# First layer of a graph network: quarter sums in seven slots a block, late tiles summed with the next group

## The chip, the cores and the metric

The kernel runs on one core of a Trainium2 chip. The metric is the device time of the whole kernel in microseconds (us), lower is better. A core has a matrix engine (PE), a vector engine (DVE), a scalar engine (ACT), a general engine (POOL, which also issues indirect gathers) and a queue engine (SP); data come and go by DMA.

## What is computed

The reference is a chain of four residual steps over 6250 nodes of 256 features and 106250 directed edges, sorted by their target node: a graph layer with edge attributes, a mixture of four experts gated by graph attention, a second graph layer, a second mixture. The change touches the first step alone:

```python
def _L0_gnn_ref(x, edge_index, edge_attr, u, batch, W1, b1, W2, b2):
    row, col = (edge_index[0], edge_index[1])
    h = jnp.concatenate([x[row], edge_attr], axis=1)
    h = jax.nn.relu(h @ W1 + b1)
    agg = jax.ops.segment_sum(h, col, num_segments=N_NODES)
    cnt = jax.ops.segment_sum(jnp.ones((h.shape[0],), h.dtype), col, num_segments=N_NODES)
    agg = agg / jnp.maximum(cnt, 1.0)[:, None]
    out = jnp.concatenate([x, agg], axis=1)
    return jax.nn.relu(out @ W2 + b2)

x = x + _L0_gnn_ref(_layernorm(x, axis=-1), edge_index, edge_attr_256, ...)
x = x + _L0_ffn_ref(_layernorm(x, axis=-1)[None], ...)[0]
x = x + _L1_gnn_ref(_layernorm(x, axis=-1), edge_weight, ..., src, dst)
x = x + _L1_ffn_ref(_layernorm(x, axis=-1)[None], ...)[0]
```

Each edge thus needs one row of x times the upper half of W1, its own attributes times the lower half, a relu, and then a sum over the edges of each target.

## The kernel before

**Tiles.** The nodes are cut into 49 blocks ("windows" in the code) of 128. The edges of a window fill 18 tiles of 128 edges. These form six runs of three tiles (`NT = 3`), k = 0 to 5, and three groups: group g has the runs g and g + 3, six tiles (`G1 = 6`). There are 147 groups, `groups1`. The table `y_dram` holds x W1's upper half for every node, so that a row of it can be gathered for each edge.

**Summing with one-hot quarters.** A window's 128 target nodes are four quarters of 32. As the edges are sorted, the edges of a tile lie in a few of them. `QUARTERS` says for each run of three tiles which: (0, 1), (0, 2), (1, 3), (1, 4), (2, 4), (3, 4), that is 1, 2, 2, 3, 2 and 1 quarters, so 33 quarter sums in 18 tiles. Edges outside these ranges are kept apart by a mask (`inside`, L1224 to L1237) and treated elsewhere. `equal` (L1270) builds the one-hot matrix `eq` on DVE, and `add_up` (L1609) multiplies: each matmul is a 128 x 32 column tile, which sums one tile's 128 rows of 257 values (256 and a one for the count) into 32 partitions of the PSUM tile `pe`. Matmuls into different quarters can run side by side, up to four of them; such a set is called a slot here. Before, a window's 12, 12 and 9 quarter sums of its three groups lie in nine slots, three for each group. The last window has whole 128-wide sums instead.

**The loop.** Iteration q does, in this order and kept so by `ordered.pin()` on each engine:

- `join(q - 1)`: DVE adds the gathered rows to the hidden product in PSUM (L1586), ACT takes the relu in place (L1587).
- `hidden(q, 0)`, later `hidden(q, 2)` and `hidden(q, 4)`: PE multiplies the transposed attributes by the lower half of W1 (L1160, `ph<-w1b,et`), two tiles at a time.
- steps of other work: the sort of the edges for the later stages, and `end_of(w)` of windows already summed (L1619 to L1663 on DVE and ACT, L1154, L1155 and L1160 for the products).
- `add_up(q - 2)`: the sums of a group joined one iteration earlier.
- `load_sources(q + 2)`: six gathers `h<-y_dram,src` on POOL (L1173) into a ring of four row buffers. The slot that they write is the one that `add_up(q - 2)` has just read, and in which the relu of that group wrote. So the first of the six waits for the group's last sum; the others have nothing more to wait for from PE.
- `turn(q + 1)`: DVE transposes the attributes (L1568, `et<-ea`).
- `load_attr`: DMAs of the attributes, issued from SP and ACT (L1477).

`eq` has three buffers. A DMA instruction can carry one wait; further ones are put into a semaphore instruction ahead of it on the same engine. On POOL there are 383 such instructions in the whole program before, 956 with the change; PE has 336 matmuls fewer, and the streams of SP and DVE stay as they were but for the masks.

`lt` (L1411) is a small bf16 tile in a later helper that writes part of the sorted order to DRAM: six times, a copy on ACT and a store from it.

Of the kernel before, what the change touches and what calls it, by code (L numbers as in the profile page):

```python
# [9 lines left out]
F32 = mybir.dt.float32  # L10
I32 = mybir.dt.int32
AF = mybir.ActivationFunctionType
OP = mybir.AluOpType
# [4 lines left out]
P = 128  # L18
# [889 lines left out]
BF16 = mybir.dt.bfloat16  # L908
# [3 lines left out]
def kernel(ctx: ExitStack, tc: tile.TileContext, a: dict, out: bass.AP):  # L912
# [10 lines left out]
    N, D = a["x"].shape  # L923
    T = -(-N // P)
# [12 lines left out]
    CW = 18  # L937
# [53 lines left out]
    with ExitStack() as fast:  # L991
# [39 lines left out]
        src1 = edges.tile([P, T, NR, NT], I32, name="src1")  # L1031
# [140 lines left out]
        def gather(dst, table, idx):  # L1172
            GP.indirect_dma_start(  # L1173
                out=dst, out_offset=None, in_=table[0:NP, :],
                in_offset=IndirectOffsetOnAxis(ap=idx, axis=0),
            )

        def load_windows(b, pool):

            sl = slice(b * TB, (b + 1) * TB)  # L1180
            n = TB * CW

            def flat3(v):
                return v.rearrange("p w a t -> p w (a t)")

            raw = {k: wix.tile([P, P], I32, name=f"raw_{k}") for k in ("src", "dst")}
            for w in range(b * TB, (b + 1) * TB):
                at, r = (w - b * TB) * CW, start_of(w)
# [38 lines left out]

            n = TB - (b == NB - 1)
            for k, (lo, hi) in enumerate(QUARTERS):
                for limit, op in ((lo * Q - 0.5, OP.is_gt), (hi * Q - 0.5, OP.is_lt)):  # L1230
                    if 0 < limit < P - 1:
                        V.scalar_tensor_tensor(
                            inside[:, :n, k, :], d[:, :n, k, :], limit, inside[:, :n, k, :],
                            op0=op, op1=OP.mult,
                        )
            if n < TB:
                V.scalar_tensor_tensor(  # L1237
                    inside[:, n, :, :], d[:, n, :, :], LAST - 0.5, inside[:, n, :, :],
                    op0=OP.is_lt, op1=OP.mult,
                )  # L1240
# [15 lines left out]
        def equal(pool, w, q):  # L1256


            total = NT * Q * sum(hi - lo for lo, hi in (quarters(w, q), quarters(w, q + NG)))
            if w < T - 1:  # L1260
                eq = pool.tile([P, EQ], F32, name="eq", bufs=3)
            else:
                eq = pool.tile([P, total], F32, name="eq4", bufs=1)
            found, at = {}, 0
            for k in (q, q + NG):
                lo, hi = quarters(w, k)
                n = (hi - lo) * Q
# [118 lines left out]
        def sorted_edges(pst, wk):  # L1386
# [19 lines left out]
            for c in range(0, KA, P):  # L1406
                n = min(P, KA - c)
                pt = pst.tile([P, 4, P], F32, name="pt")
                TE.transpose(pt[0:n, 0, :], some[:, c : c + n], ident)
                lt = wk.tile([P, P], BF16, name="lt")  # L1410
                SC.activation(lt[0:n, :], pt[0:n, 0, :], AF.Copy)  # L1411
                SC.dma_start(low_dram[c : c + n, :], lt[0:n, :])
                if c % (2 * P):
                    yield
# [7 lines left out]
        with ExitStack() as layer:  # L1422
# [114 lines left out]
            with (  # L1537
# [12 lines left out]
                last_of = [  # L1550
                    max(k % NG for k, (lo, hi) in enumerate(QUARTERS) if lo <= b < hi)
                    for b in range(4)
                ]
# [12 lines left out]

# [22 lines left out]

                def add_up(q):  # L1590

                    w, g = groups1[q]
                    if g == 0:
                        sums[w] = pse.tile([P, WS], F32, name="pe")
                    h, eq = rows_of(q), equals.pop(q)

                    for j in reversed(range(NT)):
                        for i, k in ((1, g + NG), (0, g)):
                            lo, hi = quarters(w, k)
                            if hi - lo == 4:  # L1600
                                TE.matmul(
                                    sums[w], eq[k][:, j, :], h[:, i * NT + j, 0:WS],
                                    start=g == 0 and j == NT - 1 and i == 1,
                                    stop=g == NG - 1 and j == 0 and i == 0,
                                )
                                continue
                            for b in range(lo, hi):
                                at = slice((b - lo) * Q, (b - lo + 1) * Q)
                                TE.matmul(  # L1609
                                    sums[w][b * Q : (b + 1) * Q, :], eq[k][:, j, at],  # L1610
                                    h[:, i * NT + j, 0:WS], start=g == 0 and j == NT - 1,
                                    stop=g == last_of[b] and j == 0,
                                )

                def end_of(w):

# [1180 lines left out]
```

## Time and profile before

| | us |
|---|---|
| median of three runs | 4278.34 (4271.37 to 4294.4) |
| the profiled execution | 4285.28 |
| its span | 4283.5 |
| PE busy | 3272.3 (76%) |
| POOL busy | 2257.1 (53%) |
| DVE busy | 2166.2 (51%) |
| ACT busy | 1188.7 (28%) |
| add-ups of the first layer | from 125.8 to 1539.4 us of the span |

Durations below come from the profiled execution. Its span is what the engines' records cover, 1.8 us less than its time. Views used are the page of the whole execution, tables by stretches of time, groups of instructions by line, the sums of waits, and the timelines of single engines. In a group, "idle before" is the time for which the engine did nothing just ahead of an instruction of the group, and "<-" names what ended it; "issue" means that nothing which the profile shows was being waited for. A matmul of 32-bit floats leaves two records, so 24 records are 12 matmuls.

### The profile page before, as it was taken

Reading aid. Unit: us, or ns where it says so; the run is one execution under the profiler, and the core shown is the slowest. Engines: PE = TensorE matmul, PEld = TensorE weight load, DVE = VectorE, ACT = ScalarE, POOL = GpSimd, SP = SyncE. Lnnn points to the kernel's source line nnn. Section 1 sums busy time; section 2 is a strip of 40 time slices with the busy share of each in tenths; the row PEclk is TensorE's granted clock in tenths of the full one; section 3 lists DMA queues with packets and bytes.
Section 4 is the critical chain, followed back from the end, with each engine's and each line's share of the span. In section 5 each row is a group of like instructions: output and inputs, shape, how many; then the busy total and the mean of one; then the engine's idle time right before and its main releaser. Section 6 shows DMA issues by size and latency. Waiting matters only on the chain.

```text
span 4283.5 us, 59672 instructions
## 1 busy us (share of the span) xinstructions
PE 3272.3 (76%) x19189; PEld 2500.2 (58%) x19189; DVE 2166.2 (51%) x6247; ACT 1188.7 (28%) x2203; POOL 2257.1 (53%) x2720
## 2 busy tenths in 40 slices
PE   6798888888888785777887877785346777877787
PEld 4566666666666564566665666573244555555566
DVE  7576666666555444545463544575123333333344
ACT  4122222222222232334444343463011211211123
POOL 1655655566565544345454444422666666665651
PEclk9899999999999897888998988796567667677678
DMA  5677776777676642223333332343111111111110
GB/s 172 158 172 164 167 161 157 161 171 165 159 168 153 147 108 58 61 65 100 84 99 78 81 89 67 87 109 90 45 46 52 47 51 51 50 51 48 53 47 19
DMA packets 698942, 429.43 MB, mean 100 GB/s; under 512 B 530968, under 2 KB 639563, under 8 KB 698620
## 3 DMA queue, kind: packets, MB, share of 16 engines
q0 software_dynamic: 88512, 177.73, 17.3%
q1 hardware_dynamic: 366812, 188.25, 16.4%
q10 hardware_dynamic: 243296, 59.53, 7.0%
q8 instruction: 155, 2.54, 0.3%
q14 instruction: 167, 1.37, 0.1%
HBM read 382.75 MB, written 42.50 MB: 99 GB/s over the span
## 4 chain that ended last, share of the span: by engine, by line
PE 36%; another core or an unknown queue 14%; issue 6%; DVE 5%; ACT 3%; DMA 1%; POOL 1%; DVEq 0%; ACTq 0%; SPq 0%
PE ph L1160 13%; PE py L1160 11%; PE pe L2662 5%; PE pt L1160 2%; PE po L1986 2%; PE pa L1909 1%; DVE eq L2641 1%; POOL hg L1173 1%; DVE E L1964 1%; DVE x_all L2617 1%; ACT L1787 0%; ACT hh L1787 0%; PE pe L1609 0%; PE pt L1154 0%
## 5 line engine op out<-in xcount | busy, mean ns | idle before, releaser
L1173 POOL DMA_INDIRECT h<-y_dram,src x882 | 858.4, 973 | 669.0 <-issue 485.7
L1173 POOL DMA_INDIRECT hg<-hp_dram,src x831 | 784.9, 944 | 490.7 <-issue 225.0
L1173 POOL DMA_INDIRECT sg<-gat_dram,src x612 | 593.8, 970 | 723.1 <-DVE pay L1946 313.8
L1160 PE MATMUL ph<-w1b,et 128*128 128x256 f32 x3528 | 868.2, 398 | 32.8 <-issue 26.9
L1160 PEld LDWEIGHTS ph<-w1b,et 128*128 128x128 f32 x3528 | 680.3, 198 | 204.4 <-issue 114.3
L1160 PE MATMUL py<-w,hh 128*128 128x256 f32 x1568 | 454.0, 428 | 105.6 <-issue 54.5
L2662 PEld LDWEIGHTS pe<-eq,hg 128*128 128x128 f32 x2036 | 375.3, 261 | 189.8 <-issue 117.5
L2662 PE MATMUL pe<-eq,hg 128*128 128x96 f32 (+15 forms) x2036 | 386.4, 342 | 126.2 <-issue 67.2
L1586 DVE TENSOR_TENSOR h<-ph,h 128x1536 f32<-128x1536 f32 x147 | 258.2, 1757 | 421.1 <-remote 158.6
L1160 PE MATMUL ph<-b_all,w 128*128 128x256 f32 (+1 forms) x1600 | 458.9, 426 | 11.8 <-issue 11.5
L2641 DVE TENSOR_SCALAR eq<-px,dst,ew 128x96 f32<-128x96 f32 x831 | 261.1, 367 | 320.1 <-remote 131.4
L1587 ACT ACTIVATE h<-h 128x1536 f32<-128x1536 f32 x147 | 218.2, 1484 | 728.6 <-DMA ea<-in_edge_attr_dram 288.4
L1160 PEld LDWEIGHTS py<-w,hh 128*128 128x128 f32 x1568 | 308.1, 210 | 171.1 <-issue 70.2
L1160 PEld LDWEIGHTS ph<-b_all,w 128*128 128x128 f32 x1600 | 316.9, 214 | 55.5 <-issue 17.4
L1964 DVE TENSOR_SCALAR E<-nodes,bits 128x256 bf16<-128x256 bf16 (+5 forms) x612 | 187.6, 340 | 194.4 <-remote 73.3
L1609 PE MATMUL pe<-h,eq 128*32 128x257 f32 x3168 | 256.7, 416 | 36.3 <-issue 35.2
L1568 DVE STREAM_TRANSPOSE et<-ea 128x1536 f32<-128x1536 f32 x147 | 260.5, 1773 | 12.7 <-issue 9.3
L1787 ACT ACTIVATE hh<-ph,b 128x256 f32<-128x256 f32 (+1 forms) x400 | 166.5, 467 | 306.8 <-remote 166.5
L1160 PE MATMUL py<-ew,g 65*128 65x256 f32 x392 | 146.6, 503 | 57.5 <-DVE x_all L2617 42.1
L1609 PEld LDWEIGHTS pe<-h,eq 128*32 128x32 f32 x3168 | 104.7, 116 | 143.6 <-issue 91.1
L1986 PE MATMUL po<-pays,E 128*128 128x61 bf16 x2116 | 120.0, 199 | 48.1 <-issue 41.8
L1160 PE MATMUL ph<-b_all,ew 128*128 128x512 f32 (+2 forms) x256 | 115.4, 576 | 53.4 <-ACT g L2577 33.8
(355 smaller groups left out, 3971.7 us busy)
## 6 DMA issues: line engine op xcount, KB each, us to landing
ea<-in_edge_attr_dram ACTq DMA_DIRECT2D x588, 96.0 KB
ea<-in_edge_attr_dram SPq DMA_DIRECT2D x588, 96.0 KB
w<-in_L_ffn_W_dram SPq DMA_DIRECT2D x48, 512.0 KB
y<-ys SPq DMA_DIRECT2D x96, 256.0 KB
rb<-low_dram SPq DMA_DIRECT2D x84, 256.0 KB
h<-y_dram,src POOLq DMA_INDIRECT x882
hg<-hp_dram,src POOLq DMA_INDIRECT x831
gtab<-y SPq DMA_DIRECT2D x100, 128.0 KB
```

The source lines that it names most:

```text
L1160: TE.matmul(dst, lhs(c), rhs(c), start=c == 0, stop=c == n - 1)
L1173: GP.indirect_dma_start(out=dst, out_offset=None, in_=table[0:NP, :], in_offset=IndirectOffsetOnAxis(ap=idx, axis=0),)
L1568: V.transpose(et[q].rearrange("p c m k -> p m c k"), ahead.pop(q).rearrange("p i m (c k) -> p (i m) c k", c=2),)
L1586: V.tensor_add(h, ph.pop(q), h)
L1587: SC.activation(h, h, AF.Relu)
L1609: TE.matmul(sums[w][b * Q : (b + 1) * Q, :], eq[k][:, j, at], h[:, i * NT + j, 0:WS], start=g == 0 and j == NT - 1, stop=g == last_of[b] a ...
L1787: SC.activation(hidden[u][:, f, :n, :], ph[:, f - f0, :n, :], AF.Gelu, bias=b1[:, e, f : f + 1],)
L1909: TE.matmul(pas[g][:, j, 0 : n * H], rows[g][:, j, :], part[:, i, b0 : b0 + n, :].rearrange("p t h -> p (t h)"), start=i == 0, stop=i == 2,)
L1964: V.tensor_scalar(Es[g, j][:, 0:n, :].rearrange("p b k -> p (b k)"), nodes16[:, 0 : n * P], bits.bitcast(F32)[:, g * G + j : g * G + j + 1 ...
L1986: TE.matmul(pos[g][bank][:, to * HP : (to + 1) * HP], E[:, b - b0, :], pays[g % 2][:, j, :], start=bank not in begun, stop=bank not in lat ...
L2641: V.tensor_scalar(equals[k][:, j, :], lanes[:, 0:NW], dst_of[:, t : t + 1], ew[:, t : t + 1], op0=OP.is_equal, op1=OP.mult,)
L2662: TE.matmul(sums[b][:, lo - t0 * P : hi - t0 * P], hg[:, j, :], eq[:, j, lo - n0 : hi - n0], start=False, stop=after >= (t0 + n) * P,)
```

## The change

The set of quarters is given for each tile instead of for each run of three. `RANGES` lists it in order of the 18 tiles: 26 quarter sums instead of 33. The groups of a window are taken in the order 2, 0, 1 (`TURNS`) and have 2, 2 and 3 slots (`SLOTS`), seven in all. `planned` deals the quarter sums into slots; what does not fit is left for the window's next turn, and it may be left only from the two last tiles of the two runs of a group (`LATE1`, tiles 2 and 5). The turns so have 6, 8 and 12 matmuls. As rows and one-hots of the late tiles are still needed one iteration later, the gathers are split: `load_sources(q + 1, LATE1)` gathers the two late tiles of the next group, an iteration later than before, and `load_sources(q + 2, EARLY1)` the other four. `eq` has four buffers. `lt` has one buffer; the pool's default is two.

```diff
+    TURNS, SLOTS = (2, 0, 1), (2, 2, 3)
+    RANGES = (((0, 1), 3), ((0, 2), 2), ((1, 2), 2), ((1, 3), 3), ((2, 3), 1), ((2, 4), 3), ((3, 4), 4))
+    reach = [r for r, n in RANGES for _ in range(n)]
...
-            for k, (lo, hi) in enumerate(QUARTERS):
-                for limit, op in ((lo * Q - 0.5, OP.is_gt), (hi * Q - 0.5, OP.is_lt)):
-                    if 0 < limit < P - 1:
-                        V.scalar_tensor_tensor(
-                            inside[:, :n, k, :], d[:, :n, k, :], limit, inside[:, :n, k, :],
-                            op0=op, op1=OP.mult,
-                        )
+            for limit in range(1, 4):
+                for op, some in (
+                    (OP.is_gt, [j for j in range(CW) if reach[j][0] == limit]),
+                    (OP.is_lt, [j for j in range(CW) if reach[j][1] == limit]),
+                ):
+                    part = slice(some[0], some[-1] + 1)
+                    V.scalar_tensor_tensor(
+                        tiled[0][:, :n, part], tiled[1][:, :n, part], limit * Q - 0.5,
+                        tiled[0][:, :n, part], op0=op, op1=OP.mult,
+                    )
...
-                eq = pool.tile([P, EQ], F32, name="eq", bufs=3)
+                eq = pool.tile([P, EQ], F32, name="eq", bufs=4)
...
-                lt = wk.tile([P, P], BF16, name="lt")
+                lt = wk.tile([P, P], BF16, name="lt", bufs=1)
...
-            groups1 = [(w, g) for w in range(T) for g in range(NG)]
+            groups1 = [(w, g) for w in range(T) for g in TURNS]
...
+                def planned():
+
+                    left, plan, first, final = [[] for _ in range(4)], [], {}, {}
+                    for i, g in enumerate(TURNS):
+                        for j, (k, t) in enumerate(chunk(g)):
+                            for b in range(*reach[k * NT + t]):
+                                left[b].append((i, j, k, t))
+                        for n in range(SLOTS[i]):
+                            for b in range(4):
+                                if left[b]:
+                                    plan.append((i, b, *left[b].pop(0)))
...
-                def load_sources(q):
+                def load_sources(q, some):
...
-                        gather(rows_of(q)[:, j, 0:D], y_dram, src1[:, w, k, t : t + 1])
+                        if j in some:
+                            gather(rows_of(q)[:, j, 0:D], y_dram, src1[:, w, k, t : t + 1])
...
-                    for j in reversed(range(NT)):
-                        for i, k in ((1, g + NG), (0, g)):
-                            lo, hi = quarters(w, k)
...
-                            for b in range(lo, hi):
-                                at = slice((b - lo) * Q, (b - lo + 1) * Q)
-                                TE.matmul(
-                                    sums[w][b * Q : (b + 1) * Q, :], eq[k][:, j, at],
-                                    h[:, i * NT + j, 0:WS], start=g == 0 and j == NT - 1,
-                                    stop=g == last_of[b] and j == 0,
-                                )
...
+                    for i, b, own, j, k, t, start, stop in plan:
+                        if i == turn:
+                            of = q - turn + own
+                            lo = QUARTERS[k][0]
+                            TE.matmul(
+                                sums[w][b * Q : (b + 1) * Q, :],
+                                equals[of][k][:, t, (b - lo) * Q : (b - lo + 1) * Q],
+                                rows_of(of)[:, j, 0:WS], start=start, stop=stop,
+                            )
...
                 for q in range(3):
-                    load_sources(q)
+                    load_sources(q, range(G1))
...
+                    if 3 <= q + 1 < NQ1:
+                        load_sources(q + 1, LATE1)
                     if 3 <= q + 2 < NQ1:
-                        load_sources(q + 2)
+                        load_sources(q + 2, EARLY1)
```

More of the change, by code (lines that the diff above doesn't have):

```diff
@@ L1228, in load_windows @@
             n = TB - (b == NB - 1)
-            for k, (lo, hi) in enumerate(QUARTERS):
-                for limit, op in ((lo * Q - 0.5, OP.is_gt), (hi * Q - 0.5, OP.is_lt)):
-                    if 0 < limit < P - 1:
-                        V.scalar_tensor_tensor(
-                            inside[:, :n, k, :], d[:, :n, k, :], limit, inside[:, :n, k, :],
-                            op0=op, op1=OP.mult,
-                        )
+            tiled, at = (v.rearrange("p w a t -> p w (a t)") for v in (inside, d)), 0
+            tiled = list(tiled)
+            for limit in range(1, 4):
[4 more added lines that the diff above has]
+                    part = slice(some[0], some[-1] + 1)
+                    assert len(some) == some[-1] + 1 - some[0]
+                    V.scalar_tensor_tensor(
+                        tiled[0][:, :n, part], tiled[1][:, :n, part], limit * Q - 0.5,
+                        tiled[0][:, :n, part], op0=op, op1=OP.mult,
+                    )
             if n < TB:
@@ L1548 @@
                 equals, et, ph, sums = {}, {}, {}, {}
[L1550 to L1553, printed above, removed]
+                def planned():
[8 more added lines that the diff above has]
+                                    plan.append((i, b, *left[b].pop(0)))
+                        assert all(v[0] == i and v[1] in LATE1 for some in left for v in some)
+                    assert not any(left)
+                    for n, v in enumerate(plan):
+                        first.setdefault(v[1], n)
+                        final[v[1]] = n
+                    return [
+                        (*v, n == first[v[1]], n == final[v[1]]) for n, v in enumerate(plan)
+                    ]
+                LATE1 = (NT - 1, 2 * NT - 1)
+                EARLY1 = tuple(j for j in range(G1) if j not in LATE1)
+                plan = planned()
                 NQ1 = len(groups1)
@@ L1590, in add_up @@
                 def add_up(q):
-                    w, g = groups1[q]
-                    if g == 0:
+                    w, turn = groups1[q][0], q % NG
+                    if turn == 0:
                         sums[w] = pse.tile([P, WS], F32, name="pe")
-                    h, eq = rows_of(q), equals.pop(q)
-                    for j in reversed(range(NT)):
-                        for i, k in ((1, g + NG), (0, g)):
-                            lo, hi = quarters(w, k)
-                            if hi - lo == 4:
-                                TE.matmul(
-                                    sums[w], eq[k][:, j, :], h[:, i * NT + j, 0:WS],
-                                    start=g == 0 and j == NT - 1 and i == 1,
-                                    stop=g == NG - 1 and j == 0 and i == 0,
-                                )
-                                continue
-                            for b in range(lo, hi):
-                                at = slice((b - lo) * Q, (b - lo + 1) * Q)
-                                TE.matmul(
-                                    sums[w][b * Q : (b + 1) * Q, :], eq[k][:, j, at],
-                                    h[:, i * NT + j, 0:WS], start=g == 0 and j == NT - 1,
-                                    stop=g == last_of[b] and j == 0,
-                                )
+                    if w == T - 1:
+                        for j, (k, t) in enumerate(chunk(TURNS[turn])):
+                            TE.matmul(
+                                sums[w], equals[q][k][:, t, :], rows_of(q)[:, j, 0:WS],
+                                start=turn == 0 and j == 0, stop=turn == NG - 1 and j == G1 - 1,
+                            )
+                        return
+                    for i, b, own, j, k, t, start, stop in plan:
+                        if i == turn:
+                            of = q - turn + own
+                            lo = QUARTERS[k][0]
+                            TE.matmul(
+                                sums[w][b * Q : (b + 1) * Q, :],
+                                equals[of][k][:, t, (b - lo) * Q : (b - lo + 1) * Q],
+                                rows_of(of)[:, j, 0:WS], start=start, stop=stop,
+                            )
                 def end_of(w):
```

## The prediction

> **What bounds the kernel now.** The change touches the first layer only, so I first marked that stage in the timeline: the add-ups of 144 of the 147 groups lie between 125.8 and 1539.4 us of the span, 9.82 us a group. Next the table by windows for the flat part of the stage, then the groups of instructions by line for 130 to 1540 us, then the waits, then the timelines of PE and POOL over three quiet groups.
>
> The window table (length, then busy us and instruction count of PE, PE's loads, DVE, ACT and POOL, then clock, DMA share and GB/s):
> ```profile
> 200.00:1500.00 1300.00, 1108.41 (x6807) 823.74 (x6805) 794.85 (x1467) 293.91 (x493) 770.10 (x790) 0.92 0.71 162
> ```
> PE is busy 85% of the stage and POOL 59%, so at first sight PE is the bound. The groups by line say something else (busy us, mean ns, then idle us before the instruction, and what ended it):
> ```profile
> L1160 PE MATMUL ph<-w1b,et 128*128 128x256 f32 x3433 | 841.9, 397 | 23.8 <-issue 23.1
> L1173 POOL DMA_INDIRECT h<-y_dram,src x858 | 835.0, 973 | 574.9 <-issue 478.7 <-ACT o L1155 52.1 <-ACT b_all L1155 19.5
> L1609 PE MATMUL pe<-h,eq 128*32 128x257 f32 x3163 | 255.3, 416 | 36.3 <-issue 35.2 <-DMA h<-y_dram,src 0.8
> ```
> POOL's 858 gathers take 835.0 us, and the idle time before them is 574.9 us: together 1410, the whole stretch. One gather costs 0.973 us, and 574.9 us is far more than 858 small gaps. The timeline of POOL shows where it sits (start, length, and in brackets the idle time before):
> ```profile
> 881.63 0.95 POOL L1173 DMA_INDIRECT h<-y_dram,src  x1 [0.30 <-issue]
> 884.90 0.94 POOL L1173 DMA_INDIRECT h<-y_dram,src  x1 [2.33 <-issue]
> 886.15 0.95 POOL L1173 DMA_INDIRECT h<-y_dram,src  x1 [0.30 <-issue]
> ...
> 891.16 0.95 POOL L1173 DMA_INDIRECT h<-y_dram,src  x1 [0.30 <-issue]
> 894.39 1.00 POOL L1173 DMA_INDIRECT h<-y_dram,src  x1 [2.28 <-issue]
> ```
> Six gathers of 0.95 us, five gaps of 0.30 and one hole of 2.3 make 9.5 us, and this is the period of the groups here. The timeline of PE for the same groups:
> ```profile
> 881.37 1.51 PE L1609 MATMUL pe<-h,eq 128*32 128x257 f32 x24
> 882.81 3.72 PE L1160 MATMUL ph<-w1b,et 128*128 128x256 f32 x16
> ...
> 888.63 1.50 PE L1609 MATMUL pe<-h,eq 128*32 128x257 f32 x18
> 890.06 3.72 PE L1160 MATMUL ph<-w1b,et 128*128 128x256 f32 x16
> ...
> 896.11 1.51 PE L1609 MATMUL pe<-h,eq 128*32 128x257 f32 x24
> ```
> From add-up to add-up PE needs 7.26 and 7.48 us. The sum that the gather at 884.90 waits for ended at 882.88, 2.0 us before; that of 894.39 ended at 890.13, 4.3 us before. So POOL's own cadence, hole included, is slightly the slower of the two, and PE catches up and then stands. The hole is not there where POOL found its wait done on arrival:
> ```profile
> 804.39 0.95 POOL L1173 DMA_INDIRECT h<-y_dram,src  x1 [0.30 <-issue]
> ...
> 819.28 0.95 POOL L1173 DMA_INDIRECT h<-y_dram,src  x1 [7.68 <-ACT o L1155]
> ```
> The first line begins a group and has 0.30 before it; the second shows the other case, POOL really late because PE and ACT were. I sorted the 142 starts of groups: 22 have 0.30, some 30 start 0.77 to 0.80 us after the last sum they need (PE late, gaps 2.9 to 10.6), and the other 90 or so have the hole of 2.0 to 2.3.
>
> [...]12 quarters (24 records) take 1.51 us and 9 quarters (18 records) take 1.50, so what costs is the slot of up to four, 0.50 us, not the quarter. [...]
>
> **The change part by part.** 1. Slots: nine a window become seven, so two times 48 windows = 96 fewer (the last window keeps whole sums). Below, 1.50 / 3 = 0.50 us each: 48 us of PE. By the group's busy time 255.3 / 432 = 0.59: 57 us; by the shortest reading, 0.45: 43. I take 48, a third of a microsecond a group. PE's issued matmuls fall by 336 (33 to 26 quarters a window, seven times 48).
>
> 2. What of it reaches the end? In the 112 groups with a hole or with nothing late, POOL's cadence hides it: nothing. In the 30 where PE is late the next gathers start at once with PE's signal.
>
> 3. Waits of the gathers. Before, the first of six waits for the last sum of the group. After, each waits for the last sum of its own tile. The first gather of an iteration (a late tile) is released by the first of the slots, as the leftover tiles are summed first: two or so slots earlier, 1.0 us. 30 groups by 1.0 us = 30 us. This includes the shorter add-up, for the first release comes before the dropped slots. If PE is late again by as much in the next group it is not all kept; if a shorter add-up also lets the hidden matmuls behind it run sooner, more: 20 to 45.
>
> 4. What this adds on POOL: 573 more waiting instructions (semaphore instructions on POOL go from 383 to 956), since nearly every gather now needs both PE's signal and that of the gather eight before it, and one DMA instruction carries one of them. Where both are done, 0.30 us of gap is what a gather with a finished wait shows now: nothing. Where one is not, a hole of up to 2.3 us behind five finished gathers, or none: in the stage of the GAT, gathers that carry their wait on DVE themselves follow at 0.30 in the three places where the signal came during the run; in the second layer, gathers that carry a PE wait with one more wait ahead show both 0.30 and about 2.7. So from minus 2 to plus 2.3 us a blocked wait. I take zero: the hole stays once a group, as all sums of one add-up end within 1.5 us of each other, while a hole lasts longer.
>
> 5. Late tiles gathered one iteration later: two groups ahead instead of three. Their data land some 3 us (2.4 to 6) after the issue, and the joins are 8 to 19 us after a group's last gather now; one iteration is 9.8. Most keep some microseconds; nothing, with 0 to 15 us for groups where it is short.
>
> 6. The fourth buffer of eq costs nothing on any engine. The lt tile with one buffer instead of the pool's two makes six copies on ACT wait for the store before: five waits of up to 3 us at 1422 to 1437, in a stretch where ACT stands up to 12 us; 2 us, at most 15. The tests of the ranges: six operations of 0.175 us on DVE per seven windows instead of seven; nothing. SP's and ACT's DMAs of edge attributes are the same in number and order.
>
> Sum: -30 + 2 = -28. The profiled execution took 4285.28 us (span 4283.5), so 4257.3 there; it lies 6.9 us above the median of the runs, 4278.34, so against that 4250.
>
> **The rivals.** A, the sum above: 4250, own range 4225 to 4265. B, hidden: the 30 late groups are late through the chain PE, ACT, PE of the window's end (the 7.68 us above was released by ACT), and the earlier signal only makes POOL's hole longer: 4278, 4265 to 4285. For it speaks that the periods of 9.5 us follow POOL; against it, that 30 groups do start at PE's signal.
>
> C, slower: a second hole in a group. After the late pair is released, the wait of the third gather may not yet be done when POOL's queue comes to it, and it costs another 2.3 us. The place is the turn with 12 sums, where the two pairs' signals lie farthest apart. In a third of the groups, 48 x 2.3 = 110, less 30: 4358. From 13 groups on (30 / 2.3) it eats the gain, and in all 144 it would give 4580. For it: one wait more per gather and both kinds of gap in the second layer. Against it: in quiet groups the sums were done 2 to 6 us before the gathers.
>
> D, the hole goes: waits carried by the gathers themselves[...] let POOL find waits done. Cadence then falls to 6 x 1.25 = 7.5 us, and PE binds: 1108.41 / 1300 x 9.82 = 8.37 us a group, less 0.33, is 8.04, against 9.82: at most 256 us. The trace speaks against more than half of it: where the hole was missing, POOL ran twelve gathers and PE then stood some 9 us. I take 100: 4178.
>
> **How the numbers follow.** A 0.40, B 0.18, C 0.26, D 0.16; A is likeliest, so 4250. With 0.5% (21 us, about what a measurement of this kernel can tell from no change) as the bound, A gives faster in 0.33 and no change in 0.07, B no change, C slower, D faster: 0.49, 0.25, 0.26. The range, 4165 to 4335, holds A, B, two thirds of D and a third of C, about 0.78; A's own range stands above.
>
> **What would show it.** PE's sums at about 2490 records (two to a matmul) and 205 us in the stage, gathers still 0.97 us: step 1. Holes of 2.0 to 2.3 once a group and first gathers some 0.8 us after an early sum: steps 2 to 4 as I put them. Two holes a group, or holes in the middle of the six: C. Group starts at 0.30 and PE without standing: D. ACT or DVE waiting for the late gathers' data more than the 199.5 us that the relu shows now: step 5 was wrong. I am wrong mainly if the number of holes changes, since one hole (2.3 us) weighs as much as four to five slots.

## The result and the profile after

The changed kernel takes 4416.85 us (4409.29 to 4424.11), the kernel before, beside it, 4286.37 us (4271.37 to 4295.95): 1.0308 times, with an interval of 1.0267 to 1.0348. It is slower by some 130 us where 28 us less were forecast.

Nearly all of it is in the first layer. From the first to the last of 144 add-ups the kernel before needs 1412.1 us (125.8 to 1537.9, starts), the changed one 1546.2 us (122.4 to 1668.6). That is 134.1 of the 135.9 us by which the spans differ (4419.4 and 4283.5). I split the distance between starts of add-ups by their place in the window. Before, the means are 10.99, 7.47 and 11.20 us; after, 10.33, 6.97 and 15.23. So the first two distances of each window became shorter, by 0.66 and 0.50 us, together 56 us over 48 windows. The third, from the add-up of the third turn to the first of the next window, became longer by 4.03 us, 189 us over the 47 of them.

The table by windows of the changed kernel, in the same stretch as before (columns as in the prediction):

```profile
200.00:1500.00 1300.00, 1019.09 (x5686) 754.05 (x5685) 738.47 (x1372) 271.33 (x446) 691.04 (x725) 0.88 0.67 148
```

Every engine is busy for less of the time, POOL with 691 us instead of 770, PE with 1019 instead of 1108. Nothing has become the bound by its work; the engines wait for each other. The groups by line, from 130 to 1680 us of the changed kernel:

```profile
L1163 PE MATMUL ph<-w1b,et 128*128 128x256 f32 x3460 | 880.2, 407 | 26.3 <-issue 26.1
L1176 POOL DMA_INDIRECT h<-y_dram,src x860 | 820.9, 955 | 723.2 <-issue 383.3 <-PE pe L1635 228.2 <-remote 71.4
L1635 PE MATMUL pe<-h,eq 128*32 128x257 f32 x2488 | 223.6, 440 | 15.9 <-issue 15.6
```

The sums fell from 3163 records to 2488, as forecast. POOL's idle time went up by 148 us, and 228 us of it now end with one of the sums: POOL waits for PE. Two further groups show what PE waits for, first in the kernel before, then in the changed one. L1154 (L1157 after) are the transposes at a window's end, L1661 (L1687) is ACT's copy of the gate product `wgx` out of PSUM, L1663 (L1689) its copy of the last part, `a_dst`, and L1586 (L1615) is DVE's join:

```profile
L1154 PE MATMUL pt<-ident,o 128*128 128x128 f32 x188 | 40.8, 302 | 83.9 <-ACT a_dst L1663 36.4 <-remote 22.6 <-issue 14.4
L1661 ACT ACTIVATE gtab<-pt 128x16 f32<-128x16 f32 x46 | 8.4, 183 | 162.2 <-remote 107.4 <-PE pt L1160 33.2 <-issue 18.2
L1586 DVE TENSOR_TENSOR h<-ph,h 128x1536 f32<-128x1536 f32 x144 | 253.0, 1757 | 412.4 <-remote 158.6 <-PE ph L1160 127.3 <-issue 110.6
```

```profile
L1157 PE MATMUL pt<-ident,o 128*128 128x128 f32 x190 | 48.7, 347 | 233.2 <-ACT a_dst L1689 187.5 <-remote 14.0 <-ACT gtab L1688 12.6
L1687 ACT ACTIVATE gtab<-pt 128x16 f32<-128x16 f32 x47 | 8.6, 183 | 343.3 <-remote 306.7 <-PE pt L1163 32.5 <-issue 4.1
L1615 DVE TENSOR_TENSOR h<-ph,h 128x1536 f32<-128x1536 f32 x144 | 253.0, 1757 | 486.9 <-remote 206.9 <-issue 131.8 <-PE ph L1163 127.1
```

PE stands 233 us before the transposes instead of 84, and 187.5 of it end with ACT's copies of the gate product, since the transposes need the PSUM tile that ACT is to empty. ACT in turn waits 306.7 us for something that the profile calls "remote", that is, no work of this core had ended just before the wait did. In the program this copy waits for PE's gate product and for nothing else. The timelines of one window tell the rest; first PE, then POOL, then ACT, then DVE's join, all of the changed kernel:

```profile
955.41 1.68 PE L1635 MATMUL pe<-h,eq 128*32 128x257 f32 x24
958.17 3.61 PE L1163 MATMUL ph<-w1b,et 128*128 128x256 f32 x16 [1.08 <-issue]
961.62 0.52 PE L1163 MATMUL pt<-wgx,b_all 128*128 128x24 f32 x4
961.98 1.97 PE L1163 MATMUL ph<-w1b,et 128*128 128x256 f32 x8
970.50 0.69 PE L1157 MATMUL pt<-ident,o 128*128 128x128 f32 x2 [6.55 <-ACT a_dst L1689]
```

```profile
955.75 0.95 POOL L1176 DMA_INDIRECT h<-y_dram,src  x1 [0.30 <-issue]
958.60 0.95 POOL L1176 DMA_INDIRECT h<-y_dram,src  x1 [1.91 <-PE pe L1635]
...
967.36 0.94 POOL L1176 DMA_INDIRECT h<-y_dram,src  x1 [0.30 <-issue]
972.93 0.94 POOL L1176 DMA_INDIRECT h<-y_dram,src  x1 [4.63 <-issue]
```

```profile
960.41 0.47 ACT L1648 ACTIVATE o<-pe,rc 128x256 f32<-128x256 f32 x1 [1.70 <-remote]
970.13 0.18 ACT L1687 ACTIVATE gtab<-pt 128x16 f32<-128x16 f32 x1 [9.25 <-remote]
970.21 0.17 ACT L1688 ACTIVATE gtab<-pt 128x4 f32<-128x4 f32 x1
970.27 0.18 ACT L1689 ACTIVATE a_dst<-pt 128x4 f32<-128x4 f32 x1
```

```profile
970.07 1.76 DVE L1615 TENSOR_TENSOR h<-ph,h 128x1536 f32<-128x1536 f32 x1 [9.23 <-remote]
```

PE ends the gate product at 962.14 and goes on with hidden products. ACT has been free since 960.88, but starts its copy at 970.13, 8.0 us after that end. In between POOL works through eight gathers, from 958.60 to 968.30 (the six that start from 959.85 to 966.11 are left out above). The recorded increases of PE's semaphore say the same: two are due at 961.8 and 962.1 by the ends of the matmuls, and both appear at 970.0 to 970.1, none in between. The profile's ends of matmuls are modelled, so that the delay is known only as well as these ends are. The increase due at 961.8 is that of the hidden products for which DVE's join waits, and the join was held until 970.07 as well: what is late is not one signal, but PE's signals to two engines.

So a signal of PE comes late while POOL works through a run of gathers. I measured this for the gate product in every window between 300 and 1500 us, as ACT's start less the later of PE's end and ACT being free. The mean is 2.25 us before (41 windows) and 6.38 us after (37), mostly 7.6 to 8.5, and ACT starts mostly 1.1 or 1.8 us after the run's last gather has ended. The runs themselves changed: before, 101 have six gathers and 19 have twelve; after, they have 4, 6 and 8 by turns. The eight come just after the third turn's add-up, because the late pair of the next iteration has nothing more to wait for and joins the six ahead of it.

The mean before hides two kinds of windows. In 27 of the 41 the signal is at most 0.04 us late; in the other 14 it is 0.8 to 11.1 us late, and these are exactly the windows in which POOL's last run had twelve gathers. One of them, in which the gate product ended at 862.6:

```profile
868.63 0.18 ACT L1661 ACTIVATE gtab<-pt 128x16 f32<-128x16 f32 x1 [7.06 <-remote]
```

So late signals are not new with the change. It brought them into nearly every window: in 35 of the 37 the signal is now 1.1 us late or more.

### The profile page after: what moved, and what is told of

Read it like the earlier page. It is cut to its first block, busy times and chain, and to the rows that moved or that the text cites. A ratio compares the mean times of both kernels' runs of the same rounds, so it can differ in the third digit from the quotient of the medians.

```text
span 4419.4 us, 58897 instructions
## 1 busy us (share of the span) xinstructions
PE 3252.0 (74%) x18517; PEld 2471.9 (56%) x18517; DVE 2162.8 (49%) x6240; ACT 1191.2 (27%) x2203; POOL 2236.5 (51%) x2720
## 3 DMA queue, kind: packets, MB, share of 16 engines
q8 instruction: 150, 2.46, 0.2%
## 4 chain that ended last, share of the span: by engine, by line
PE 41%; another core or an unknown queue 19%; issue 12%; DVE 9%; ACT 5%; DMA 2%; POOL 2%; ACTq 1%; SPq 0%; DVEq 0%; POOLq 0%
PE ph L1163 18%; PE py L1163 9%; PE pe L2690 4%; PE pe L1635 3%; PE pt L1163 3%; PE po L2014 1%; POOL hg L1176 1%; PE pt L1157 1%; ACTq L1486 1%; DVE h L1615 1%; DVE eq L2669 1%; ACT L1815 1%; DVE et L1597 1%; DVE E L1992 1%
## 5 line engine op out<-in xcount | busy, mean ns | idle before, releaser
L1176 POOL DMA_INDIRECT h<-y_dram,src x882 | 842.3, 955 | 813.1 <-issue 389.7
L1163 PE MATMUL ph<-w1b,et 128*128 128x256 f32 x3528 | 898.2, 408 | 35.6 <-issue 26.1
L1163 PEld LDWEIGHTS ph<-w1b,et 128*128 128x128 f32 x3528 | 701.0, 204 | 225.3 <-issue 128.2
L1615 DVE TENSOR_TENSOR h<-ph,h 128x1536 f32<-128x1536 f32 x147 | 258.2, 1757 | 496.1 <-remote 206.9
L2690 PE MATMUL pe<-eq,hg 128*128 128x96 f32 (+15 forms) x2036 | 373.2, 334 | 138.5 <-issue 74.9
L2690 PEld LDWEIGHTS pe<-eq,hg 128*128 128x128 f32 x2036 | 362.0, 253 | 201.6 <-issue 124.0
L1635 PE MATMUL pe<-h,eq 128*32 128x257 f32 x2496 | 225.5, 440 | 18.4 <-issue 18.1
L1157 PE MATMUL pt<-ident,o 128*128 128x128 f32 x196 | 49.9, 345 | 233.2 <-ACT a_dst L1689 187.5
L1157 PEld LDWEIGHTS pt<-ident,o 128*128 128x128 f32 x196 | 28.0, 168 | 256.8 <-ACT a_dst L1689 200.2
```

The costliest lines, as they stand in the source:

```text
L1157: TE.transpose(pt[:, c, :], src[:, c * P : (c + 1) * P], ident)
L1163: TE.matmul(dst, lhs(c), rhs(c), start=c == 0, stop=c == n - 1)
L1176: GP.indirect_dma_start(out=dst, out_offset=None, in_=table[0:NP, :], in_offset=IndirectOffsetOnAxis(ap=idx, axis=0),)
L1615: V.tensor_add(h, ph.pop(q), h)
L1635: TE.matmul(sums[w][b * Q : (b + 1) * Q, :], equals[of][k][:, t, (b - lo) * Q : (b - lo + 1) * Q], rows_of(of)[:, j, 0:WS], start=start, s ...
L2690: TE.matmul(sums[b][:, lo - t0 * P : hi - t0 * P], hg[:, j, :], eq[:, j, lo - n0 : hi - n0], start=False, stop=after >= (t0 + n) * P,)
```

## Experiments

Three theories were put to the test. A: late signals of PE behind POOL's runs make the loss. B: each added wait and signal has its price. C: the uneven turns of sums. (These letters are not those of the prediction's rivals.) The chips differed much. "Ratio" below is always to the kernel before on the same chip, whose median is given; expectations in us were written for the first chip, at 4286 us. The changed kernel itself was run on the first chip and on those at 3348 and 4284 us. On those at 4214 and 4273 us it was not, so that its loss there is taken from the others.

**Early tiles first.**

```diff
+                    if 3 <= q + 2 < NQ1:
+                        load_sources(q + 2, EARLY1)
                     if 3 <= q + 1 < NQ1:
                         load_sources(q + 1, LATE1)
-                    if 3 <= q + 2 < NQ1:
-                        load_sources(q + 2, EARLY1)
```

> The changed kernel with the two lines of gathers swapped: in each iteration the four early tiles of the group after next are gathered first, then the two late tiles of the next group. The same 26 sums in seven slots; waits of POOL fall from 956 to 719 semaphore instructions. Theory A (PE's signals reach the other engines only when POOL's unbroken run of gathers has ended, and the run of eight gathers lies over the signal of the gate product, L1163 wgx to ACT L1687): the runs become 6, 6, 6, ACT sees the gate product at once in most windows, PE's wait at L1157 for a_dst falls from 188 us to under 60, time 4230 to 4300. Theory B (the price lies in the many waits and signals of single sums): a third of the added waits is gone, so a third of the loss: about 4375. Theory C (the uneven turns of 6, 8 and 12 sums): nothing changes, 4417.

Measured: 4201.97 us, before 4214.2: 0.9990 (0.9966 to 1.0013). No loss is left. PE's transposes and ACT's copy of the gate product:

```profile
L1157 PE MATMUL pt<-ident,o 128*128 128x128 f32 x188 | 38.8, 289 | 35.3 <-issue 10.1 <-ACT a_dst L1689 7.6 <-DVE start L1084 7.4
L1687 ACT ACTIVATE gtab<-pt 128x16 f32<-128x16 f32 x47 | 8.6, 182 | 68.7 <-PE pt L1163 25.3 <-remote 19.1 <-issue 18.8
```

The wait for a_dst is 7.6 instead of 187.5 us, and the signal's mean delay 0.35 us. C is out, since the sums and turns are those of the change; this supposes that the changed kernel would lose on this chip, for which the late signals of the run with the gate product moved, below, speak. B would have kept almost three fifths of the loss, as 336 of the 573 added waits stay. The swap changes order and waits at once, so it does not tell which of them made the signals late.

**Many waits in the kernel before.**

```diff
-                    for j, (k, t) in enumerate(chunk(g)):
-                        gather(rows_of(q)[:, j, 0:D], y_dram, src1[:, w, k, t : t + 1])
+                    tiles = list(enumerate(chunk(g)))
+                    for n in (5, 2, 4, 1, 3, 0):
+                        j, (k, t) = tiles[n]
+                        gather(rows_of(q)[:, j, 0:D], y_dram, src1[:, w, k, t : t + 1])
```

> The kernel before with its six gathers of a group issued in the order in which their tiles are summed, so that each waits for its own sum: semaphore instructions on POOL rise from 383 to 1098, more than with the change, sums and slots stay. Theory A (held signals behind runs of eight): runs stay at six, so no loss of the size seen: 4270 to 4320. Theory B (price of waits and signals): a loss as large as the change's or larger, 4420 to 4450. Theory C (uneven turns): 4286.

Measured: 4225.83 us, before 4214.2: 1.0021 (0.9994 to 1.0048). With 1098 semaphore instructions on POOL, more than in the changed kernel's 956, there is hardly a loss. B falls. The gate signal's delay is 1.04 us in the mean.

**Runs of eight in the kernel before**, with its few waits:

```diff
-                    if 3 <= q + 2 < NQ1:
-                        load_sources(q + 2)
+                    both = [(q + 2, (0, 1, 3, 4)), (q + 1, (2, 5))]
+                    if (q - 2) % NG == 0:
+                        both.reverse()
+                    for n, some in both:
+                        if 3 <= n < NQ1:
+                            load_sources(n, some)
```

> The kernel before, its nine slots and its 383 semaphore instructions on POOL as they are, but with two gathers of each group issued an iteration later, placed so that POOL's runs are 6, 8 and 4 gathers as in the changed kernel, the eight behind the window's last add-up. Theory A (held signals): most of the loss comes without a single wait added: 4370 to 4430, with PE's wait for a_dst up from 36 to 150 us or more. Theory B (price of waits): 4286. Theory C (uneven turns of sums): 4286.

Measured: 4220.71 us, before 4214.2: 1.0014 (0.9989 to 1.0038). The profile has 38 runs of four, 37 of six and 45 of eight, and still:

```profile
L1154 PE MATMUL pt<-ident,o 128*128 128x128 f32 x188 | 37.4, 282 | 16.4 <-issue 6.7 <-remote 4.7 <-ACT order L1369 4.6
```

No wait for a_dst is among the first three, and the signal's delay is 0.19 us. This was a miss of theory A as I had it: the length of the run alone does not make the signal late. In most windows the gate product ended less than 1.1 us after the run's start here. But in nine windows it ended 1.8 to 5.2 us after, and all nine had their signal at once. Two other windows had it 2.8 and 4.8 us late.

**Gate product one step earlier**, gathers and waits as changed:

```diff
                     transposed(psm, b_all[:, w, :], xn)
                     yield
-                    yield
                     pg = psm.tile([P, D], F32, name="pt")
```

> The changed kernel with one step fewer between a window's transposed rows and its gate product, so that PE makes the gate product one stretch of hidden products earlier. Gathers, waits and sums are untouched. Theory A (held signals): a signal that comes within some 2 us of the start of POOL's run still gets through, so part of the windows lose their wait: PE's wait for a_dst falls to 60 to 130 us and the time to 4330 to 4390. Theories B (price of waits) and C (uneven turns): 4417, no change.

Measured: 4259.3 us, before 4214.2: 1.0130 (1.0046 to 1.0213), where the changed kernel has 1.0308 and 1.029 on other chips.

```profile
L1157 PE MATMUL pt<-ident,o 128*128 128x128 f32 x190 | 40.1, 294 | 76.9 <-ACT a_dst L1688 24.2 <-remote 9.6 <-ACT o L1648 9.6
```

Not a wait of POOL was touched, and by the medians more than half of the loss is gone (by the upper end of the interval, from four runs, a third): that part ran over this one signal. What is left may run over PE's signal to DVE, whose join now waits 288.6 us for "remote" (206.9 in the changed kernel, on another chip); this was not tested. It did not come about as expected, either. The signal is still late (3.48 us in the mean), in windows with the product 1.1 to 2.5 us after the run's start too; PE merely needs it later.

With run length and number of waits each harmless where tried alone in the kernel before, the next experiment kept order and runs of the changed kernel and took the waits away. Inside each pair and each four, the gather of the tile summed last goes first; the others then have nothing more to wait for.

```diff
-                    for j, (k, t) in enumerate(chunk(g)):
-                        if j in some:
+                    last = {(own, j): n for n, (_, _, own, j, *_) in enumerate(plan)}
+                    order = sorted(some, key=lambda j: -last[(q - 4) % NG, j])
+                    tiles = list(enumerate(chunk(g)))
+                    for j in order if q >= 4 else some:
+                        k, t = tiles[j][1]
+                        if True:
                             gather(rows_of(q)[:, j, 0:D], y_dram, src1[:, w, k, t : t + 1])
```

> The changed kernel with late tiles still first, runs of gathers still 4, 6 and 8 and released by the same early sums, but inside each pair and each four the gather of the tile summed last comes first, so that the others have no wait of their own: semaphore instructions on POOL fall from 956 to 526. Theory A2 (PE's signals are late where a long run of gathers meets gathers that carry PE waits of their own): the gate product's signal gets through, 0.985 to 1.005 of the kernel before. Theory A1 (the order alone, late pair first and so a run of eight that begins before the add-up ends): nothing changes, 1.025 to 1.035. Theory B (a fixed price for each wait): 430 of 573 added waits gone, 1.005 to 1.012.

Beside it ran the changed kernel as it is, and two versions with the early tiles first and few waits (the first of them has the late pair first in one turn of three, which keeps the runs of eight).

> The changed kernel itself, once more, so that it stands beside the runs of this call on one chip. All theories: 1.025 to 1.035 times the kernel before.

> The changed kernel's sums and slots, with the early four first where the late pair has sums to wait for and the late pair first where it has none: runs of 4, 6 and 8 gathers as with the change, and the last-summed tile first: 431 semaphore instructions on POOL. Theory A2 (long runs together with own waits): 0.98 to 1.005, as in the kernel before with such runs. Theory A1 (run length and order): 1.015 to 1.035.

> The changed kernel's sums and slots with early tiles first and, among them, the tile summed last first: runs of six, one wait for PE an iteration, 384 semaphore instructions on POOL, that is the kernel before in its waits, with seven slots for nine. All theories: no loss. If the shorter add-ups are worth what the prediction took (a third of PE's saving reaching the end): 0.99 to 0.996; if POOL's cadence hides them all: 0.998 to 1.002; if the holes of POOL are what the own waits saved: 1.00 to 1.01.

These runs met a chip on which the kernel before takes 3348.47 us. Measured there, as ratios: the changed kernel 0.9968 (0.9955 to 0.9981), late first with few waits 0.9966 (0.9951 to 0.9980), runs of eight with few waits 1.0050 (1.0034 to 1.0065), early first with few waits 1.0064 (1.0047 to 1.0081). The expectation for the changed kernel missed. The other three results lie in one of the ranges named, but they tell no theories apart, because what these speak of is not there. The changed kernel on this chip, its window table from 200 to 1200 us, then its groups from 130 to 1260 us:

```profile
200.00:1200.00 1000.00, 953.67 (x5924) 742.57 (x5924) 761.96 (x1410) 281.20 (x473) 735.64 (x758) 0.98 1.02 202
```

```profile
L1176 POOL DMA_INDIRECT h<-y_dram,src x859 | 832.1, 969 | 295.2 <-issue 184.3 <-PE pe L1635 54.9 <-DMA h<-y_dram,src 25.9
L1157 PE MATMUL pt<-ident,o 128*128 128x128 f32 x190 | 37.4, 279 | 23.5 <-ACT o L1676 9.4 <-ACT lt L1420 8.4 <-ACT key L1378 3.1
L1687 ACT ACTIVATE gtab<-pt 128x16 f32<-128x16 f32 x47 | 8.6, 184 | 80.8 <-PE pt L1163 80.8
```

A gather costs the same 0.97 us. But POOL's holes are gone (295 us idle in 859 gathers, that is little over 0.30 each), the gate signal's delay is 0.03 us, and PE is busy 95% of the time. The change is worth 0.3% there. The granted clock in the stage is higher too, 0.98 against 0.92 in the kernel before on the first chip, so that the chips differ in more than the signals.

It is not the gate product's signal alone. Of 995 increases that PE's semaphore was due between 200 and 1200 us on this chip, one is recorded more than 0.5 us after its matmul's end. On the first chip, between 200 and 1500 us, it is 304 of 513 in the kernel before and 424 of 949 in the changed one. This is a rough count, as the records of the first chip lack 97 of the 513 increases and 77 of the 949. It fits what the windows with twelve gathers show: late signals are there in both kernels, and the change decides on which work they fall.

The pair that matters was therefore run again:

> The changed kernel once more. In the call before, on a chip on which the kernel before takes 3348 us, POOL had no holes and the gate product's signal was never late. Theory A3 (the loss is made of late signals, and these are a property of the chip in use): on a chip on which the kernel before takes 4200 us or more, 1.02 to 1.035 times it, with the gate product's signal late by 6 us or more in the mean; on one at 3350 us, 0.995 to 0.999 and no late signal.

> The changed kernel with late tiles first as in the change, but with the tile summed last first inside each pair and each four, so that POOL has 526 instead of 956 semaphore instructions; runs and order of tiles otherwise as changed. On a chip at 4200 us or more: theory A2 (own waits of the gathers make PE's signals late) 0.985 to 1.005; theory A1 (the order, a run of eight that begins before the add-up ends) 1.02 to 1.035; theory B (a fixed price for each wait) 1.005 to 1.012. On a chip at 3350 us it can't tell them apart: 0.995 to 0.999.

Measured, with the kernel before at 4283.87 us: the changed kernel 4401.36 us, 1.0290 (1.0235 to 1.0344); with few waits 4280.87 us, 1.0004 (0.9986 to 1.0022). First the changed kernel's groups in these runs, then those of the version with few waits (L1691 is its copy of the gate product):

```profile
L1157 PE MATMUL pt<-ident,o 128*128 128x128 f32 x190 | 49.5, 352 | 245.1 <-ACT a_dst L1689 186.6 <-remote 39.2 <-DVE ix_g L1212 5.2
L1687 ACT ACTIVATE gtab<-pt 128x16 f32<-128x16 f32 x47 | 8.6, 183 | 345.5 <-remote 318.3 <-PE pt L1163 24.2 <-issue 3.0
```

```profile
L1157 PE MATMUL pt<-ident,o 128*128 128x128 f32 x190 | 45.3, 326 | 135.8 <-remote 74.7 <-ACT a_dst L1693 30.2 <-ACT key L1378 8.3
L1691 ACT ACTIVATE gtab<-pt 128x16 f32<-128x16 f32 x47 | 8.6, 183 | 291.1 <-remote 256.8 <-PE pt L1163 28.6 <-issue 5.6
```

Both have 4, 6 and 8 gathers by turns (45, 45, 45 and 46, 46, 47 runs). Without the own waits of most gathers the signal's mean delay falls from 6.70 to 3.81 us; it is mostly given 2.4 to 2.7 us before the run of eight ends, not after it. PE's wait for a_dst falls from 187 to 30 us, though of the 245 us that PE stands before the transposes 136 remain. The third distance between add-ups falls from 15.06 to 12.60 us: 2.46 over 47 of them is 115 us, of the 132 us by which the stage differs in the two profiled executions; the medians differ by 120 us. The gate product ends as long after the start of a run of eight in both (3.04 and 3.12 us, medians), so that it is not a shift of one against the other.

The last two runs looked for a version faster than both:

> The version with late tiles first and few own waits (526 semaphore instructions), and in addition the gate product one step earlier. If PE's remaining wait behind late gate signals (mean delay 3.8 us in the version without this step) still costs time on a chip at 4200 us or more: 0.985 to 0.997 of the kernel before. If POOL's cadence binds by then: 0.998 to 1.003. On a chip at 3350 us no signal is late and the step is worth nothing: 0.995 to 0.999.

> The changed kernel with the early four gathered before the late two, as run before at 0.999 of the kernel before on a chip at 4214 us. On a chip at 4200 us or more: 0.996 to 1.002 again. On a chip at 3350 us, where the same order with few waits took 1.006: if the order is what costs there (the late pair's rows come later), 1.004 to 1.008; if the waits were, 0.995 to 0.999.

Measured, with the kernel before at 4273.02 us: 4287.68 us, 1.0028 (1.0010 to 1.0046), and 4256.0 us, 0.9963 (0.9941 to 0.9985). The first is one of the two outcomes named, and not the one hoped for: the earlier gate product gains nothing once the waits are few. The second, early tiles first, is the best of those tried on chips of this kind: 0.9963 here and 0.9990 on the chip at 4214 us, where the interval takes in no change; on the faster chip it was run only with few waits, and lost 0.6%.

## Why the prediction was wrong

**The bound.** That POOL's cadence with a hole of 2.3 us paces the stage beside PE fits the runs. What the reading had wrong is what the hole is. In its example the sum ended at 890.13 and POOL's last gather at 892.11, but PE's increase is recorded at 893.66, and the next gather starts 0.73 us behind that. Between 200 and 1500 us the kernel before has 79 holes of 1.8 to 2.6 us in which POOL waited for PE. In 61 of them the sum had ended before the run's last gather, by 2.2 us (median); yet POOL's wait ended mostly 1.3 to 1.6 us after that gather, just behind a recorded increase of PE. So the hole is itself a late signal of PE, and on the chip without holes one of 995 signals was more than 0.5 us late. I had taken the hole as a cost of POOL alone. Yet the kernel before already showed ACT waiting 107 us for "remote" at L1661, with a free ACT and a finished PE. That line I did not read, and rival D's remark that PE stood where POOL had run twelve gathers concerns the very windows with a late gate signal.

**Step 1, slots.** Right in number (2488 records for 2490), short in worth: busy time fell by 31.7 us, not 48, because the mean of a record rose from 416 to 440 ns. A slot cost what was taken: in the add-ups at 881.37 us before and 955.41 after the records start in fours, within 0.02 us of each other, and the next four 0.20 to 0.24 us later; 8 sums in two slots took 1.07 us, 12 in three 1.51 (medians). But the sums' records that start while the granted clock is 0.5 took 0.63 us in the mean, the others 0.385 before and 0.386 after; of the first kind there are 405 in 3168 before and 546 in 2496 after. Most of these are in the turn with six sums, the first after the third distance, whose two slots took 1.94 us (median of 46). With the gate product one step earlier the same sums took 201.9 us at 404 ns, near the 205 forecast, though on another chip; so the shortfall is not one of the slots. That it comes with the late signals is my estimate.

**Steps 2 and 3.** The first two distances of a window did become shorter, by 56 us, more than the 30 us forecast for the whole. So the gain was there, and was given back more than three times in the third distance.

**Step 4 failed.** I took zero for the 573 waits, "the hole stays once a group", and bounded a wait between minus 2 and plus 2.3 us on POOL. On POOL this was not far off: between 200 and 1500 us 3 of the 120 groups have two gaps of more than 1 us before gathers, 115 have one. In both traces each of the 2325 gathers carries one wait or none, and the records of semaphore instructions on POOL are 394 and 967, the 573 more that were counted. But I asked only what a wait costs the engine that waits. The price was paid elsewhere, by PE's signal to ACT: 4.03 us a window, through ACT's copy and PE's PSUM tile, 189 us. On the chip at 4284 us, with the order of the change kept, the kernel took 1.0290 with these waits and 1.0004 without most of them. Rival B had named the chain PE, ACT, PE of the window's end, but only as a place where sums are late already; step 4 did not put it on the path.

**Step 5.** Not a cost, as forecast: the relu's waits for gathered rows fell from 199.5 us to 48.6. The longer third distance gave the rows more time, so this is no clean test; with few waits and no loss they were 173.4 us.

**Step 6.** About right: ACT waits 4.1 us in all for stores of lt where 2 were taken. The lt tile with two buffers was not tried beside four of eq, so that this rests on the trace alone.

**The rivals.** C had the direction and the place, the turn with 12 sums, and asked for 4358. Its mechanism, a second hole on POOL, is not what happened, so that its direction was right for another reason. D's picture, POOL without holes, came true in a way not meant, with 295 us idle before 859 gathers instead of 574.9 before 858: by the chip, not by the change.

What stays open: why PE's signals come late behind POOL's gathers on some chips and not on others (mean delay of the gate signal 6.70 and 0.03 us with the same kernel), and why the loss takes both the order with the late pair first and many own waits. Many waits in the kernel before, without that order, took 1.0021; that order without the many waits 1.0004; many waits in the changed kernel with the order turned, 0.9990. As far as these runs go the loss needs both; they do not show how the two act. Nor do they show which late signals get through: in the kernel before with runs of eight nearly all gate signals did.

## What to carry to other kernels

Waits put on one engine can go with late signals of another: on the chip at 4284 us 956 semaphore instructions on POOL went with a mean delay of 6.70 us of PE's gate signal, 526 with 3.81. When waits are added to an engine that issues runs of gathers, look also at who else waits for the same producer, and how far behind its end he starts. If several instructions wait for results of one burst, let the first wait for the last result, so that the others wait for nothing; on that chip it took 430 waiting instructions away and all of the loss. An idle time that the profile ends with "remote" while the producer is long done is a warning: 107.4 us at ACT's copy in the kernel before already, 306.7 with the change.

## What was unexpected in the hardware

- PE's signals come late while POOL issues gathers: the gate product's by up to 8.9 us in the changed kernel and up to 11.1 us in the kernel before, behind a run of twelve. In the changed kernel ACT sees it mostly 1.1 or 1.8 us after the end of the run's last gather, and in the kernel before POOL sees that of the sums mostly 1.3 to 1.6 us after it.
- This differs from chip to chip. The three chips of the experiments with the kernel before at 4214 to 4284 us show it (mean delays up to 3.48, 2.23 and 6.70 us in the versions run there), one at 3348 us does not (0.03 us). Each chip of the experiments was used in one set of runs only, so that it may be a state of the chip and not the chip. With it go the holes of POOL, though the gather itself takes 0.97 us on both kinds.
- The sign of the change goes with it: 1.029 on one kind, 0.9968 on the other.
